# Ten hc tiles for the selective scan of images 1 to 3 where there were six, four of them in a second pool opened behind the last scan inputs

## The chip, the cores and the metric

The kernel runs on one core of one Trainium2 chip. The metric is the device time of one execution in microseconds. A core has five engines with their own queues, each of which runs its instructions in the order in which they were written into it: TensorE (PE; its weight loads are listed as PEld), VectorE (DVE), ScalarE (ACT), GpSimd (POOL) and SyncE (SP), which here only starts transfers. SBUF is the working memory, PSUM the memory that matmuls write to.

## What is computed

Four images of 64 x 64 tokens with 128 channels pass through four layers. Layer 0 is a selective scan block: layer norm, an input projection, a 3 x 3 depthwise convolution, then in each of four directions a recurrence over 4096 tokens for 256 channels x 16 states, and after it a norm, a gate, an output projection and an MLP. Layer 1 is attention of every token to every token, layer 2 a block of convolutions, layer 3 attention over a 7 x 7 neighbourhood and an MLP. The part of layer 0 that matters here:

```python
def step(h, t):
    x_t, d_t, B_t, C_t = t
    h = jnp.exp(d_t[..., None] * A) * h + (d_t * x_t)[..., None] * B_t[:, :, None, :]
    return (h, jnp.einsum('bkdn,bkn->bkd', h, C_t))
_, ys_l = jax.lax.scan(step, h0, scan_in)
```

## The kernel before

The program is written as plain loops, and a scheduler puts the instructions of each engine in order before the kernel runs. It does so with a planned time of its own and with priorities: the scan's instructions are traced under `priority(tc, K, SCAN_FIRST)` with a very large number, so that they come after whatever else is ready, and fill what the other layers leave free. The order is fixed in the program; on the chip each engine follows it and waits where an operand or a buffer is not ready.

`network` (L1624) first makes the scan's pools (`make_scan`, L410), then `scan_inputs` of image 0 (L277). Then come, for images 0 to 3, the scan of the image (`selective_scan`, L438) and beside it other work: beside the scan of image 0 the scan inputs of images 1 to 3, and beside the scan of image i (1 to 3) `rest` (L1594) of image i - 1, which is scan output (L565), layer 1 (L715), layer 2 (L911) and layer 3's attention (L1222). Layer 3's MLP of an image is run within the scan output of the next. `rest` of image 3 has no scan beside it and stands at the end; its scan output (`scan_over`) takes the space of the scan's pools.

The scan of one image runs over four directions (`ORDER`), eight chunks of 512 tokens, two halves of the channels, four groups of states (`j`) and two parts (`pp`). Each turn of the innermost loop is called a unit here: 512 units for an image, 2048 in all. For one unit:

- GpSimd makes `dB` (128 x 2 x 512) from `du` and a row of B (L485), into one of four tiles.
- ScalarE makes `dA = exp(dt * A)` twice (L491), into one of three PSUM banks.
- VectorE runs the recurrence twice (L493). Where the unit's number is in `ON_POOL`, it writes into the unit's `hc` tile, and GpSimd multiplies the tile by a row of C two units later (L506). Otherwise it writes over `dA`, and VectorE makes the product into `hc` (L498). For images 1 to 3, 7 of 16 units are GpSimd's.
- ScalarE keeps the last column as the state of the next chunk (L500, L502).
- PE sums the states: for each `j`, eight (as the trace counts them) passes `py <- hc, pick` for two units (L539), which read the two `hc` tiles and set them free. At the first `j` a matmul with `y_before` opens the sum (L524, L527, L534), at the last the sum is copied out of PSUM (L549, L556) before `py`, a single bank, can be opened again.

`hc` is a tile of 4 KB per partition; there are six. A seventh unit's recurrence or product must wait for a py matmul. The matmuls of the other layers stand between py matmuls on PE: in layer 1 the score and value matmuls (L781, L829), in layer 2 two blocks of five 3 x 3 convolutions (L247, called from layer 2), in layer 3 the scores (L1287, L1291) and the values and sums (L1307), in 64 groups an image, each opened by two L1287 instructions. In scan output they are L602 to L640.

Of the kernel before, what the change touches and what calls it, by code (L numbers as in the profile page):

```python
# [28 lines left out]
F32 = mybir.dt.float32  # L29
# [13 lines left out]
LC = 512  # L43
# [24 lines left out]
def mid(ap, n):  # L68

    return bc(ap.unsqueeze(1), [ap.shape[0], n, ap.shape[1]])  # L70
# [29 lines left out]
class Together:  # L100
# [3 lines left out]
    def __init__(self, tc, K):  # L104
        self.tc, self.K, self.done = tc, K, None
# [57 lines left out]
def loader(tc, pool, A, layer):  # L163
    def load(name, shape, src=None):
        t = pool.tile(shape, F32, name=f"w{layer}_{name}")
        tc.nc.sync.dma_start(t, A[f"L{layer}_conv_{name}"] if src is None else src)
        return t

    return load
# [95 lines left out]
def make_conv_diagonals(tc, K, A, out):  # L265
    nc = tc.nc
    with tc.tile_pool(name="mk_conv", bufs=1) as pool:
        convw = pool.tile([128, ND, 9], F32, name="convw")
        nc.sync.dma_start(convw, A["L0_conv_conv_w"])
        diag = pool.tile([128, ND, 9, 128], F32, name="conv_diag")  # L270
        for d in range(ND):
            for t in range(9):
                nc.scalar.activation(diag[:, d, t, :], K.ident, AF.Copy, scale=convw[:, d, t : t + 1])
        nc.sync.dma_start(out, diag)
# [135 lines left out]
def make_scan(ctx, tc, K, A):  # L410

    nc = tc.nc
    S = SimpleNamespace()
    big = ctx.enter_context(tc.tile_pool(name="ss_big", bufs=1))
    S.pool = ctx.enter_context(tc.tile_pool(name="ss", bufs=2))
    S.psum = ctx.enter_context(tc.tile_pool(name="ss_ps", bufs=1, space=PSUM))
    load = loader(tc, big, A, 0)
    S.A = load("A_log", [128, KD, NJS, NPR, 2])
    nc.scalar.activation(S.A, S.A, AF.Exp)
    nc.vector.tensor_scalar_mul(S.A, S.A, -1.0)  # L420
    ds4 = load("Ds", [128, ND, KD])
    total = big.tile([128, ND], F32, name="Dsum")
    nc.vector.tensor_reduce(total, ds4, AX.X, ALU.add)
    S.skip = big.tile([128, ND, 128], F32, name="skip_diag")
    for d in range(ND):
        nc.scalar.activation(S.skip[:, d, :], K.ident, AF.Copy, scale=total[:, d : d + 1])

    S.pick = big.tile([128, 32], F32, name="pick")
    nc.gpsimd.memset(S.pick, 1.0)
    for base, sign in ((0, 1), (3, -1)):  # L430
        nc.gpsimd.affine_select(
            S.pick, S.pick, [[-4 * sign, 32]], ALU.is_ge, 0.0, base=base, channel_multiplier=sign
        )
    S.unit = 0
    return S


def selective_scan(tc, K, S, D, img):  # L438
# [6 lines left out]


    nc = tc.nc
    pool, psum = S.pool, S.psum
    waiting = []

    def settle(unit):
        while waiting and waiting[0][0] <= unit:
            waiting.pop(0)[1]()

    for k in ORDER:
# [4 lines left out]
        for i in range(NCH):  # L460
            c = NCH - 1 - i if back else i
            for hf in range(2):
# [11 lines left out]
                for j in range(NJS):  # L474
# [7 lines left out]
                    for pp in range(2):  # L482
                        pr = 2 * hf + pp
                        dB = pool.tile([128, 2, LC], F32, name="dB", bufs=4)
                        nc.gpsimd.tensor_mul(dB, dus[pp], mid(bt, 2))  # L485
                        on_pool = S.unit % 16 in ON_POOL[img > 0]
                        S.unit += 1
                        hc = pool.tile([128, 2, LC], F32, name="hc", bufs=6)
                        for g in range(2):
                            dA = psum.tile([128, LC], F32, name="dA", bufs=3)  # L490
                            nc.scalar.activation(dA, dts[pp][:, g, :], AF.Exp, scale=S.A[:, k, j, pr, g : g + 1])  # L491
                            hg = hc[:, g, :] if on_pool else dA
                            nc.vector.tensor_tensor_scan(  # L493
                                hg[:, order], dA[:, order], dB[:, g, order],
                                0.0 if i == 0 else state[:, j, pr, g : g + 1], ALU.mult, ALU.add,
                            )
                            if not on_pool:
                                mm = nc.vector.tensor_mul(hc[:, g, :], dA, ct)  # L498
                                if i < NCH - 1:
                                    nc.scalar.copy(state[:, j, pr, g : g + 1], dA[:, last : last + 1])  # L500
                        if on_pool and i < NCH - 1:
                            nc.scalar.copy(state[:, j, pr, :], hc[:, :, last])  # L502
                        if on_pool:

                            def product(hc=hc, ct=ct, made=made):
                                made.append(nc.gpsimd.tensor_mul(hc, hc, mid(ct, 2)))  # L506

                            waiting.append((S.unit + BEHIND, product))
                        else:
                            made.append(mm)  # L510
                        hcs.append(hc)
                        settle(S.unit)
# [1111 lines left out]
def network(tc, A, out):  # L1624
    nc = tc.nc
    with ExitStack() as ctx:
        nc.scalar.preload_act_table_set("natural_log_exp_and_others")
        K = make_consts(ctx, tc)
        dram = ctx.enter_context(tc.tile_pool(name="scratch", bufs=1, space=DRAM))

        def scratch(name, shape):
            return dram.tile(shape, F32, name=f"{name}_dram")

        D = SimpleNamespace()
        D.bias = scratch("bias", [len(BIAS_KINDS), 128, HEADS * 512])
        D.biasT = [[scratch(f"biasT{k}_{i}", [128, HEADS, LC]) for i in range(4)] for k in range(3)]
        D.conv_diag = scratch("conv_diag", [128, ND, 9, 128])
        D.w2_diag, D.w2_norms = scratch("w2_diag", [128, 20, 128]), scratch("w2_norms", [128, len(NORMS2), 4])
        D.w2_cv4, D.w2_bias = scratch("w2_cv4", [128, 128]), scratch("w2_bias", [1, 128])
        for name, shape in (("sz", [128, ND, LC]), ("xc", [128, ND, LC]), ("y", [128, ND, LC])):  # L1640
            setattr(D, name, [[scratch(f"{name}{b}_{c}", shape) for c in range(NCH)] for b in range(B)])
        for name, shape in (("delta", [128, ND, LC]), ("du", [128, ND, LC]), ("bc", [NS, 2, LC])):
            made = [
                [[scratch(f"{name}{b}_{k}_{c}", shape) for c in range(NCH)] for k in range(KD)] for b in range(B)
            ]
            setattr(D, name, made)
        D.y_first = [[[scratch(f"y_first{b}_{k}_{c}", [128, ND, LC]) for c in range(NCH)] for k in range(2)] for b in range(B)]
        D.y_cols = [scratch(f"y_cols{b}", [NCH, 128, NCH, ND, RC * RC]) for b in range(B)]
        for name in ("x4", "x5"):
            setattr(D, name, [scratch(f"{name}_{b}", [NT, C]) for b in range(B)])  # L1650
        D.shift = [scratch(f"shift{b}", [NJ, 128]) for b in range(B)]

        with ExitStack() as scan_ctx:
            S = make_scan(scan_ctx, tc, K, A)
            make_conv_diagonals(tc, K, A, D.conv_diag)
            with priority(tc, K, SCAN_FIRST // 2):
                with tc.tile_pool(name="mk_w2", bufs=1, side="right") as pool:
                    make_layer2(tc, K, A, D, pool)
            scan_inputs(tc, K, A, D, 0)
            before = None  # L1660
            for img in range(B):
                with priority(tc, K, SCAN_FIRST):
                    selective_scan(tc, K, S, D, img)
                if img == 0:
                    make_bias(tc, K, A, D.biasT)
                    for later in range(1, B):
                        scan_inputs(tc, K, A, D, later)
                else:
                    rest(tc, K, A, D, img - 1, before)
                    before = img - 1, out[img - 1]  # L1670
            rest(tc, K, A, D, B - 1, before, scan_ctx.close)
            layer3_mlp_alone(tc, K, A, D, B - 1, out[B - 1], 8)
        needed = ctx.enter_context(tc.tile_pool(name="needed", bufs=1)).tile([1, 1], mybir.dt.int32, name="needed")
        bound_exceeded(tc, K, needed)
        with tc.If(nc.values_load(needed) > 0):
            everything_again(tc, K, A, D, out)
# [80 lines left out]
```

## Time and profile before

| | us |
|---|---|
| median of 3 runs | 8911.95 |
| lowest and highest run | 8906.75, 8919.55 |
| profiled execution, span | 8926.7 |
| PE busy in it | 7138.8 (80%) |
| VectorE busy | 7119.8 (80%) |
| GpSimd busy | 7048.6 (79%) |
| ScalarE busy | 5642.5 (63%) |

The span runs from the first to the last instruction of one execution that was taken with the profiler on; it is 15 us over the median of the runs. For the time of the profiled execution only this span is known. The scan of image 0 takes about the first 2200 us, that of each further image some 1850 us, the last py matmul is at 7804 us, and the rest of image 3 follows without GpSimd. GpSimd's share of 79% is therefore near 90% over the time in which it has work. In a row of a group the two numbers after the bar are the busy time in all (us) and the mean of one (ns), and what follows the second bar is how long the engine stood idle before them and what ended most of that. In a row of stretches the columns are the stretch, its length, the busy time and the count of instructions of PE, PEld, DVE, ACT and POOL, the mean granted clock of TensorE as a share of its full speed, the busy share of the DMA engines and GB/s.

### The profile page before, as it was taken

How to read it: one execution, taken by the hardware profiler on the slowest of the kernel's cores; microseconds unless marked ns; L12 is line 12 of the kernel's file. 1: busy time of each engine (PE TensorE's matmuls, PEld its weight loads, DVE VectorE, ACT ScalarE, POOL GpSimd, SP SyncE). 2: the span in 40 equal slices, each digit the busy share in tenths (PEclk: the TensorE clock that was granted, in tenths of full speed). 3: DMA queues.
4: the chain of work that ended last, by engine and by line, in shares of the span. 5: the costliest groups of instructions: out<-in, count | busy, mean ns of one | idle time of the engine just before them, and what ended most of it. 6: DMA issues, size and time to landing. Idle time of an engine off the chain costs nothing. (4 is left out here: it accounts for less than half of the span.)

```text
span 8926.7 us, 101201 instructions
## 1 busy us (share of the span) xinstructions
PE 7138.8 (80%) x30116; PEld 2711.7 (30%) x30116; DVE 7119.8 (80%) x8483; ACT 5642.5 (63%) x11581; POOL 7048.6 (79%) x3064
## 2 busy tenths in 40 slices
PE   6835868687788997887788988777888888888987
PEld 2211213132332232333322232333322333343333
DVE  3888878888899989998899989988999889813433
ACT  5646767676576666667766666657766666654355
POOL 5988898989899989998899979987899889900000
PEclk8756868697799998888899998888899988999989
DMA  5777676777554546566444555565544555520020
GB/s 174 249 236 239 227 252 239 266 240 266 188 168 165 170 150 222 188 205 201 164 165 164 179 180 195 191 208 171 166 167 169 169 198 194 173 69 4 7 79 29
DMA packets 864124, 1581.89 MB, mean 177 GB/s; under 512 B 219702, under 2 KB 344781, under 8 KB 859214
## 3 DMA queue, kind: packets, MB, share of 16 engines
q1 hardware_dynamic: 733261, 1399.17, 47.0%
q10 hardware_dynamic: 130304, 176.19, 5.5%
q8 instruction: 240, 3.93, 0.2%
q14 instruction: 319, 2.61, 0.1%
HBM read 1280.47 MB, written 283.59 MB: 175 GB/s over the span
## 5 line engine op out<-in xcount | busy, mean ns | idle before, releaser
L485 POOL TENSOR_TENSOR dB<-du,b_rows 128x1024 f32<-128x1024 f32 x2048 | 4801.3, 2368 | 622.9 <-DVE hc L493 184.8
L491 ACT ACTIVATE dA<-dt,w_A_log 128x512 f32<-128x512 f32 x4096 | 2784.7, 690 | 636.5 <-DVE hc L493 353.1
L493 DVE TENSOR_TENSOR_SCAN dA<-dA,state,dB 128x512 f32<-128x512 f32 x2128 | 2634.8, 1272 | 231.0 <-ACT dA L491 136.3
L493 DVE TENSOR_TENSOR_SCAN hc<-dA,state,dB 128x512 f32<-128x512 f32 x1456 | 1802.5, 1268 | 263.6 <-PE py L539 117.2
L506 POOL TENSOR_TENSOR hc<-hc,c_rows 128x1024 f32<-128x1024 f32 x832 | 1969.3, 2367 | 52.7 <-issue 23.9
L498 DVE TENSOR_TENSOR hc<-dA,c_rows 128x512 f32<-128x512 f32 x2432 | 1567.9, 676 | 115.0 <-PE py L539 97.5
L539 PE MATMUL py<-hc,pick 128*32 128x512 f32 x8192 | 1244.7, 686 | 367.3 <-POOL hc L506 270.7
L500 ACT COPY state<-dA 128x1 f32<-128x1 f32 x2128 | 327.5, 158 | 1220.4 <-DVE hc L498 1211.8
L829 PE MATMUL pa<-e,l_v 128*128 128x512 f32 x2048 | 1062.0, 650 | 16.8 <-ACT e L785 16.2
L781 PE MATMUL pair<-l_g,l_f 32*128 32x512 f32 x2048 | 530.5, 667 | 198.3 <-ACT e L785 146.9
L785 ACT ACTIVATE e<-pair 128x1024 f32<-128x1024 f32 (+1 forms) x448 | 508.4, 1135 | 225.7 <-PE pair L781 220.3
L829 PEld LDWEIGHTS pa<-e,l_v 128*128 128x128 f32 x2048 | 374.2, 199 | 668.5 <-issue 621.1
L539 PEld LDWEIGHTS py<-hc,pick 128*32 128x32 f32 x8192 | 209.5, 116 | 1114.7 <-issue 476.7
L247 PE MATMUL ps<-band,w_conv_diag 128*128 128x504 f32 (+3 forms) x1152 | 503.5, 596 | 6.7 <-ACT delta L397 6.5
L1287 PE MATMUL pair<-table,ident 128*128 128x512 f32 x768 | 414.3, 665 | 111.4 <-ACT e L1297 79.1
L493 DVE TENSOR_TENSOR_SCAN dA<-dA,dB 128x512 f32<-128x512 f32 x304 | 356.2, 1213 | 76.2 <-POOL dB L485 57.4
L328 POOL TENSOR_TENSOR du<-delta,xc 128x1024 f32<-128x1024 f32 x128 | 335.4, 2630 | 52.0 <-ACT delta L397 45.3
L1297 ACT ACTIVATE e<-pair 128x1024 f32<-128x1024 f32 (+1 forms) x224 | 254.3, 1135 | 155.6 <-PE pair L1291 155.6
L201 PE MATMUL ps<-ident,ln_xn 128*128 128x128 f32 x512 | 134.2, 360 | 263.9 <-ACT ln_xn L198 214.3
L219 PE MATMUL ps<-xnT,w_fc_w 128*128 128x512 f32 x512 | 266.6, 656 | 62.9 <-ACT xnT L202 22.7
L233 PE MATMUL ps<-mlp_h,w_fc_w 128*128 128x512 f32 x512 | 275.8, 683 | 42.6 <-ACT mlp_h L226 42.6
L247 PEld LDWEIGHTS ps<-band,w_conv_diag 128*128 128x128 f32 x1152 | 221.6, 194 | 288.7 <-issue 260.4
(274 smaller groups left out, 8400.0 us busy)
## 6 DMA issues: line engine op xcount, KB each, us to landing
b_rows<-bc_dram SPq DMA_DIRECT2D x1024, 256.0 KB
c_rows<-bc_dram SPq DMA_DIRECT2D x1024, 256.0 KB
dt<-delta_dram SPq DMA_DIRECT2D x512, 512.0 KB
du<-du_dram SPq DMA_DIRECT2D x512, 512.0 KB
delta_dram<-delta ACTq DMA_DIRECT2D x128, 512.0 KB
du_dram<-du SPq DMA_DIRECT2D x128, 512.0 KB
table<-biasT_dram SPq DMA_DIRECT2D x72, 512.0 KB
y_first_dram<-y_sum ACTq DMA_DIRECT2D x128, 256.0 KB
```

The lines of the kernel that those rows point to most:

```text
L247: mm = nc.tensor.matmul(out[:, r0 - row0 : r1 - row0, c0:c1], lhsT((dy + 1) * 3 + dx + 1), src[:, r0 + dy : r1 + dy, c0 + dx : c1 + dx], s ...
L328: nc.gpsimd.tensor_mul(du.rearrange("p d (a b) -> p d a b", b=H), deltas[b].rearrange("p d (a b) -> p d a b", b=H), tk,)
L485: nc.gpsimd.tensor_mul(dB, dus[pp], mid(bt, 2))
L491: nc.scalar.activation(dA, dts[pp][:, g, :], AF.Exp, scale=S.A[:, k, j, pr, g : g + 1])
L493: nc.vector.tensor_tensor_scan(hg[:, order], dA[:, order], dB[:, g, order], 0.0 if i == 0 else state[:, j, pr, g : g + 1], ALU.mult, ALU.add,)
L498: mm = nc.vector.tensor_mul(hc[:, g, :], dA, ct)
L506: made.append(nc.gpsimd.tensor_mul(hc, hc, mid(ct, 2)))
L539: mm = nc.tensor.matmul(py[0][32 * q : 32 * q + 32, :], S.pick, hcs[q // 2][:, q % 2, :], start=(k == 1 and j == 0), stop=(j == NJS - 1),)
L781: nc.tensor.matmul(ps[:, u, :], f[quad, t // 4, span(t % 4, 128)], g[quad, c, :], start=True, stop=True)
L785: made = nc.scalar.activation(e, ps, AF.Exp)
L829: nc.tensor.matmul(pa, v[:, 8 * q + t, :], es[q], start=(t == 0 and q == 0), stop=(t == 7 and q == 3),)
L1287: nc.tensor.matmul(ps[:, u, :], K.ident, t[:, u, :], start=True, stop=False)
```

## The change

The scan asks an object for its `hc` tiles. For the scan of image 0 and for the first 40 tiles of image 1, it takes them from the old ring of six. After that it takes four of every ten from a pool `ss_more`, opened after the scan inputs of image 3 have been traced and so at the address where their pools began, and six of every ten from the old ring; each tile is then used again ten units later. The pool stays open until the scan's other pools close, so that the pools of `rest` for images 0 to 2 start 16 KB per partition higher. The branch of the program that runs everything again in a general form does not use the second pool.

```diff
@@ make_scan
     S.unit = 0
+    S.products = Products(S.pool)
     return S
+class Products:
+
+    def __init__(self, pool):
+        self.pool, self.more, self.turn = pool, None, 0
+
+    def widen(self, pool, bufs):
+        self.more, self.bufs, self.turn = pool, bufs, -40
+
+    def tile(self):
+        self.turn += 1
+        if self.more is not None and self.turn > 0 and self.turn % (6 + self.bufs) < self.bufs:
+            return self.more.tile([128, 2, LC], F32, name="hc", bufs=self.bufs)
+        return self.pool.tile([128, 2, LC], F32, name="hc", bufs=6)
@@ selective_scan
-    pool, psum = S.pool, S.psum
+    pool, psum, products = S.pool, S.psum, S.products
...
-                        hc = pool.tile([128, 2, LC], F32, name="hc", bufs=6)
+                        hc = products.tile()
@@ network
                     for later in range(1, B):
                         scan_inputs(tc, K, A, D, later)
+                    more = scan_ctx.enter_context(tc.tile_pool(name="ss_more", bufs=1))
+                    S.products.widen(more, 4)
```

## The prediction

> **What bounds the kernel now.** I read the busy shares first, then the groups, then what VectorE waits for, then busy times cut at the stages of the layers that run beside the scan, and last the timeline of one such stage and of the scan's end. The page's span and its costliest groups of the scan:
>
> ```profile
> span 8926.7 us, 101201 instructions
> ...
> L485 POOL TENSOR_TENSOR dB<-du,b_rows 128x1024 f32<-128x1024 f32 x2048 | 4801.3, 2368 | 622.9 <-DVE hc L493 184.8
> ...
> L506 POOL TENSOR_TENSOR hc<-hc,c_rows 128x1024 f32<-128x1024 f32 x832 | 1969.3, 2367 | 52.7 <-issue 23.9
> ```
>
> A scan unit (one dB, one hc tile) costs GpSimd one L485 and, in 7 of 16 units for images 1 to 3, one L506: 2.368 + 7/16 x 2.367 = 3.40 us. The waits that the change aims at, over the whole run (microseconds, times, longest):
>
> ```profile
> DVE hc L493 <- PE py L539: 118.8, 67, 6.3
> ...
> DVE hc L498 <- PE py L539: 97.5, 48, 8.1
> ```
>
> Asked stage by stage, images 1 to 3 hold 134 us of these 216, and 124 of the 134 lie beside layer 1 (60) and layer 3 (64). What GpSimd does there is the next view: busy time of PE, PEld, DVE, ACT and POOL in stretches cut at the stages (layer 1, layer 2, layer 3 of image 0; scan output of image 1; layer 3 of image 2 up to the last py matmul).
>
> ```profile
> 2540.00:3245.00 705.00, 628.65 (x2642) 194.61 (x2640) 663.33 (x704) 474.58 (x897) 699.18 (x302) 0.96 0.51 172
> 3245.00:3385.00 140.00, 131.53 (x444) 56.64 (x444) 109.05 (x136) 85.91 (x171) 89.97 (x40) 0.95 0.39 124
> 3385.00:4000.00 615.00, 500.08 (x2712) 183.46 (x2712) 562.33 (x640) 391.08 (x834) 596.87 (x258) 0.86 0.63 207
> 4000.00:4445.00 445.00, 340.94 (x1336) 162.10 (x1336) 379.67 (x535) 318.98 (x710) 359.62 (x156) 0.83 0.55 180
> ...
> 7225.00:7804.00 579.00, 468.72 (x2536) 177.24 (x2536) 534.27 (x613) 365.35 (x768) 557.99 (x241) 0.86 0.60 200
> ```
>
> GpSimd is 99% busy beside layer 1 and 97% beside layer 3: there a VectorE wait for an hc tile costs nothing, since the next dB is not there anyway. It idles beside layer 2 (50 of 140 us) and scan output (85 of 445). Layer 2's gaps, GpSimd and then PE in order of time (start, length, idle before in brackets):
>
> ```profile
> 3305.03 4.72 POOL L485 TENSOR_TENSOR dB<-du,b_rows 128x1024 f32<-128x1024 f32 x2 [20.34 <-DVE hc L493]
> ...
> 3343.45 2.36 POOL L485 TENSOR_TENSOR dB<-du,b_rows 128x1024 f32<-128x1024 f32 x1 [21.00 <-PE ps L979]
> ```
>
> ```profile
> 3264.62 32.16 PE L247 MATMUL ps<-l_h,w_diag 128*128 128x448 f32 x90
> ```
>
> Twice a stage (the second time from 3304.72) PE runs 32 us of convolution with no py matmul, so no hc tile comes free, the scan stops, and GpSimd stands for 20 us. This happens six times. The run's end, PE:
>
> ```profile
> 7823.58 1.98 PE L1287 MATMUL pair<-table,ident 128*128 128x512 f32 x4 [1.12 <-ACT e L1297]
> ...
> 7828.41 1.98 PE L1287 MATMUL pair<-table,ident 128*128 128x512 f32 x4
> ...
> 7836.66 1.16 PE L1324 MATMUL pj<-w_proj_w,oT 128*128 128x128 f32 x8 [0.26 <-DVE oT L1320]
> 7851.09 6.50 PE L602 MATMUL ps<-y,center 128*128 128x512 f32 x8 [13.27 <-DMA y<-y_dram]
> ```
>
> Layer 3 of image 2 ends at 7838, 34 us after the last py matmul, and only then does the tail begin (its weights and y are loaded into space that this layer 3 held): 8927 - 7838 = 1089 us that the change does not touch. So the end is the end of layer 3 of image 2, plus a constant.
>
> **The Trainium skill.** "Perfetto Trace Analysis", section Optimization Strategy, says that a gap repeating on the engine that should be saturated can mean that there isn't enough SBUF or PSUM for the next tile. The trace agrees in layer 2 (six gaps of about 20 us), and shows in the other stages that a wait for a tile on another engine than the bound is no such gap. The same page, Sequencer Loop, has each instruction wait in its engine's queue; the trace agrees: py matmuls stand behind 90 convolution passes. "GPSIMD Engine Reference", section 3.1, gives 4497 ns for a GpSimd and 2293 ns for a VectorE product of 2048 f32; here 2367 ns for 1024 against 2 x 676 for VectorE's L498, so GpSimd is indeed the dear side of the unit.
>
> **The change part by part.** It adds and removes no arithmetic. The first 40 hc tiles of image 1 are as before. The new pool lies where the scan inputs' pools lay, but their last matmul stands ahead of unit 512 on PE, and its first tile comes at unit 553: no wait; taken as 0. The pools of the later layers move up by 16 KB per partition; layer 3's last e tile then shares space with xT, whose last read (layer 2) comes before: 0.
>
> What does change is the planned order. I counted, in both built programs, how many scan units stand before each stage's first instruction on ScalarE (before / after): layer 1 of image 0 starts 597/596.5; layer 2 805/808.5, ends 829/838; scan output of image 1 1014.5/1024.5, ends 1115/1124.5; layer 2 1327.5/1339 to 1351/1367.5; scan output of image 2 1540/1557 to 1638/1659; layer 2 1855.5/1876.5 to 1879/1903.5; scan ends at 2048 in both. So the scan is planned ahead of the layers by 24.5 units at the end. And after the last py matmul PE has 6 groups of layer 3's 64 (two L1287 instructions each) before, 16 after.
>
> Price by stage:
>
> - Layer 1 and layer 3, GpSimd-bound, 3.43 us per unit (3.40 / 0.99): layer 1 +4, +2, 0 units; layer 3 +1, +0.5, -24.5: -17 units, -58 us. Counted on PE it is +6, +2, +4, +2, 0, -24: -10 units, -34 us. ScalarE's count sets when an exponential may run, PE's when a py matmul may; I take the middle, -46.
> - Layer 2: +5.5, +5, +3.5 units at no GpSimd time, hidden by the 20 us gaps. But PE is 94% busy there. Its extra py matmuls are 5 units x 0.53 us (1.06 us for the 8 passes of two units), and in four of the six convolutions a y_before matmul now stands behind the first 9 or more of 45 instructions, 1.1 us and an unknown wait for the last y_sum copy: from 0 to 8 us. I take 4 us a stage, +12; ends 0 and +36.
> - Scan output: -0.5, -0.5, +4 units. GpSimd is 81% busy here; what orders the stage is ScalarE and VectorE between layers' steps (VectorE's hc waits are only 7 us in the three). Free at best, 3 x 3.40 = 10 at worst; I take +5.
> - Layer 3's hc waits, 64 us: nearly all covered by GpSimd. Its idle time there is some 20 us a stage; I take -5; ends -12 and 0.
> - Left of layer 3 after the scan: 10 groups more. Two starts of one above are 4.83 us apart, the pair before 4.16: 4.5 us, so 45; with one chunk's q, k, v and two ends of chunks, on paths now uncovered, about 9 more: +54; ends +45 and +65. Beside the scan the same group took 615 / 64 = 9.6 us, but cost nothing, as GpSimd set the pace.
>
> Sum: -46 + 12 + 5 - 5 + 54 = +20 us. Against the profiled span, 8926.7 + 20 = 8947; the runs' median, 8912, is 15 us (0.16%) under that span, so 8932. All ends together: -58 + 0 + 0 - 12 + 45 = -25 and -34 + 36 + 10 + 0 + 65 = +77.
>
> **Rivals.** (1) Gaps filled for nothing, ends faster. The place is layer 2: 14 units run inside its six convolutions, the stage stays at 140 us, the scan is done 58 + 12 us early, and the 16 left groups cost only their 45: -25, 8887. For it: GpSimd's and VectorE's 31 and 50 us of idle time in that stage. Against: PE is full there, and the scan's lead must be paid in layer 3 left over. It decides if the last py matmul comes more than 54 us earlier. (2) A draw: the 124 us of waits under a full GpSimd were never paid, and lead and leftover cancel within 18 us: 8912. For it: my two counts differ by 24 us, as much as the result. (3) Broken convolutions: the y_before matmuls inside wait for ScalarE's copy and stall PE in a stage that it bounds, +36 in place of +12, and the shorter lead counted on PE holds: +56, 8968. For it: L527 already waits 36 us for y_sum copies. Against: copies are planned before. (4) The change does nothing since the new tiles come late: excluded from unit 553 on by the count above.
>
> **How the numbers follow.** Forecast, slower by 10 to 40 us: 0.36. Rival 3 and beyond: 0.12. Draw: 0.29. Rival 1: 0.21. Rival 4: 0.02. About 0.2%, 18 us, is what a measurement can tell. Slower by more than that: most of the forecast's case and all of rival 3, 0.45; faster, 0.22 (rival 1 and a little beyond); within, the draw, rival 4 and the forecast's low edge, 0.33. The likeliest case gives 8932; the range takes in rival 1's 8887 and rival 3's 8968: 8885 to 8972. The likeliest case's own range is 8922 to 8952.
>
> **What would show it.** In the profile after: the 20 us gaps of GpSimd in layer 2 shorter than 12 us; layer 1 and layer 3 still with GpSimd above 96%; the waits for py on VectorE mostly gone with no gain from it; the last py matmul 20 to 45 us earlier; and layer 3 of image 2 running 80 to 100 us past it instead of 34, with 1089 us behind. I am wrong if layer 3's leftover is short, if GpSimd's idle time in scan output falls, or if layer 2 grows by over 10 us.

## The result and the profile after

The change makes the kernel faster by a fifth of a per cent: 8898.9 us median of 20 runs (8888.4 to 8915.7), against 8916.9 us for the kernel before beside it (20 runs, 8906.8 to 8946.4). The ratio is 0.9977, 95% interval 0.9970 to 0.9984. The forecast was 8932 us. The profiled execution is the slowest of the 20, 16.8 us over their median; its span is 12.7 us under that of before.

Lines of the kernel after are 16 higher from L485 on (dB L501, recurrence L509, VectorE's product L514, GpSimd's product L522, py L555, layer 3's scores L1303). The page after, span and the scan's two groups of GpSimd:

```profile
span 8914.0 us, 101143 instructions
...
L501 POOL TENSOR_TENSOR dB<-du,b_rows 128x1024 f32<-128x1024 f32 x2048 | 4817.8, 2389 | 553.6 <-DVE hc L509 137.0
...
L522 POOL TENSOR_TENSOR hc<-hc,c_rows 128x1024 f32<-128x1024 f32 x832 | 1988.6, 2390 | 34.7 <-issue 16.1
```

What VectorE waits for, after (us, times, longest):

```profile
DVE hc L514 <- PE py L555: 61.1, 19, 8.2
...
DVE hc L509 <- PE py L555: 26.4, 9, 6.3
```

The waits for tiles fell from 216 to 88 us. To see which of that counted, I cut both traces at the first TensorE instruction of each stage (L602, L749, L950, L1249 of the kernel before) and read the busy times between the cuts. GpSimd idles for a row's length less the fifth busy time. First the kernel before: layer 3 of image 0, layer 3 of image 2 up to the last py matmul, and the rest up to the start of image 3's scan output.

```profile
3383.60:4018.30 634.70, 509.69 (x2750) 186.59 (x2750) 581.99 (x662) 399.64 (x848) 613.95 (x266) 0.86 0.63 206
...
7228.40:7804.40 576.00, 469.12 (x2537) 177.35 (x2538) 530.87 (x610) 363.20 (x763) 554.75 (x240) 0.87 0.60 200
7804.40:7851.10 46.70, 29.02 (x165) 10.79 (x165) 2.42 (x6) 7.96 (x9) 0.00 (x0) 0.88 0.21 58
```

And after: layers 1, 2 and 3 of image 0, the scan output of image 1, and the last two as above.

```profile
2570.10:3271.20 701.10, 628.91 (x2616) 192.07 (x2617) 664.45 (x708) 468.12 (x893) 698.21 (x303) 0.94 0.53 172
3271.20:3415.50 144.30, 133.91 (x469) 58.14 (x470) 125.15 (x150) 93.47 (x189) 110.71 (x48) 0.97 0.48 154
3415.50:4040.30 624.80, 494.87 (x2744) 185.29 (x2745) 582.22 (x664) 396.63 (x834) 615.21 (x267) 0.87 0.65 210
4040.30:4461.30 421.00, 326.21 (x1310) 159.61 (x1311) 360.26 (x516) 315.10 (x716) 344.22 (x149) 0.84 0.55 181
7223.20:7709.30 486.10, 394.95 (x2112) 145.56 (x2112) 454.01 (x521) 309.64 (x646) 473.63 (x205) 0.85 0.60 198
7709.30:7829.70 120.40, 86.61 (x486) 36.82 (x487) 6.32 (x18) 26.41 (x39) 0.00 (x0) 0.85 0.22 65
```

Three things are to be seen. Layer 3 of image 0 holds as much GpSimd work as before (614 and 615 us), and takes 10 us less: its idle time went from 21 to 10 us. In layer 3 of image 2 the scan ends 95 us earlier (7804 to 7709). And of these 95 us, 74 are given back at once: the rest of layer 3, with nothing of GpSimd beside it, grows from 47 to 120 us.

As GpSimd's work in all is constant (7049 and 7044 us up to there), the start of image 3's scan output is that work plus GpSimd's idle time. All stages of the three images together, idle us of GpSimd:

| | before | after |
|---|---|---|
| up to the first scan output | 289.6 | 297.0 |
| scan output | 223.6 | 218.4 |
| layer 1 | 21.6 | 12.7 |
| layer 2 | 150.9 | 109.1 |
| layer 3 beside the scan | 70.0 | 28.6 |
| layer 3 left over after the scan | 46.7 | 120.4 |
| sum | 802.4 | 786.2 |
| scan output of image 3 starts | 7851.1 | 7829.7 |

So the change takes 97 us of idle time away in four kinds of stage, and adds 74 at the end and 7 before the first scan output. The short stalls that went in layer 3 can be seen in what GpSimd waits for there; image 1, before and then after:

```profile
POOL dB L485 <- DVE hc L493: 10.9, 3, 8.1
POOL dB L485 <- issue: 4.4, 1, 4.4
POOL hc L506 <- issue: 3.8, 1, 3.8
POOL hc L506 <- ACT state L502: 2.6, 1, 2.6
```

```profile
POOL dB L501 <- DMA sz<-sz_dram: 2.7, 1, 2.7
POOL dB L501 <- DVE hc L509: 2.1, 2, 1.2
POOL dB L501 <- DMA b_rows<-bc_dram: 1.5, 1, 1.5
```

Two of these stalls, 4.4 and 3.8 us, come right after waits of VectorE for py (4.7 and 3.7 us): with six tiles a late py matmul holds VectorE's recurrence up, and GpSimd stands until that is done. The longest, 8.1 us, is of another kind: VectorE stood before a MEMSET of the next scan output (L584). VectorE and GpSimd in order of time:

```profile
5817.85 2.46 DVE L493 TENSOR_TENSOR_SCAN hc<-dA,state,dB 128x512 f32<-128x512 f32 x2 [4.68 <-PE py L539]
...
5820.44 2.36 POOL L485 TENSOR_TENSOR dB<-du,b_rows 128x1024 f32<-128x1024 f32 x1 [4.42 <-issue]
...
5929.29 0.27 DVE L584 MEMSET center<- 128x256 f32 x1 [8.92 <-issue]
...
5933.91 2.35 POOL L485 TENSOR_TENSOR dB<-du,b_rows 128x1024 f32<-128x1024 f32 x1 [8.13 <-DVE hc L493]
```

The idle times named "issue" have no releaser in the profile. Over the three layers 3, the idle time of GpSimd that lies under a wait of VectorE for py, or begins within 3 us of its end, is 22 of the 70 us before and none of the 29 after; in the layers 1 it is 6 of 22 and none of 13. So some 28 of the 50 us that went stood beside the waits that the change aims at. The other 22 went elsewhere in these stages, in part at their ends; these traces don't show by what.

What is paid at the end, TensorE after the last py matmul of the kernel after:

```profile
7710.84 0.51 PE L1323 MATMUL den<-e,ones 128*32 128x192 f32 x8
7712.06 1.12 PE L1338 MATMUL pj<-bias_row,ones 1*128 1x512 f32 x2 [0.71 <-ACT rec L1333]
...
7723.72 1.63 PE L201 MATMUL ps<-ident,ln_xn 128*128 128x128 f32 x4 [5.50 <-ACT ln_xn L198]
...
7734.10 3.78 PE L1303 MATMUL pair<-table,ident 128*128 128x512 f32 x4 [0.67 <-ACT v L1297]
...
7814.46 1.16 PE L1340 MATMUL pj<-w_proj_w,oT 128*128 128x128 f32 x8 [0.26 <-DVE oT L1336]
7829.71 2.90 PE L618 MATMUL ps<-y,center 128*128 128x512 f32 x3 [14.10 <-DMA y<-y_dram]
```

Sixteen groups of layer 3 are left (64 passes of L1303, four a group, fall after the last py matmul; 24, so six groups, before). Between 7711 and 7734 stands one chunk's layer norm and its q, k and v, which the scan covered before.

### The profile page after: what moved, and what is told of

It reads as the page before. It is cut to its first block, busy times and chain, and to the rows that moved or that the text cites. A ratio compares the mean times of both kernels' runs of the same rounds, so it can differ in the third digit from the quotient of the medians.

```text
span 8914.0 us, 101143 instructions
## 1 busy us (share of the span) xinstructions
PE 7120.9 (80%) x30116; PEld 2708.4 (30%) x30116; DVE 7132.4 (80%) x8483; ACT 5640.4 (63%) x11581; POOL 7043.5 (79%) x3064
## 5 line engine op out<-in xcount | busy, mean ns | idle before, releaser
L501 POOL TENSOR_TENSOR dB<-du,b_rows 128x1024 f32<-128x1024 f32 x2048 | 4817.8, 2389 | 553.6 <-DVE hc L509 137.0
L509 DVE TENSOR_TENSOR_SCAN dA<-dA,state,dB 128x512 f32<-128x512 f32 x2128 | 2634.8, 1275 | 242.6 <-POOL dB L501 129.4
L522 POOL TENSOR_TENSOR hc<-hc,c_rows 128x1024 f32<-128x1024 f32 x832 | 1988.6, 2390 | 34.7 <-issue 16.1
L509 DVE TENSOR_TENSOR_SCAN hc<-dA,state,dB 128x512 f32<-128x512 f32 x1456 | 1805.4, 1270 | 218.8 <-ACT dA L507 134.6
L514 DVE TENSOR_TENSOR hc<-dA,c_rows 128x512 f32<-128x512 f32 x2432 | 1568.2, 679 | 76.1 <-PE py L555 61.1
L555 PE MATMUL py<-hc,pick 128*32 128x512 f32 x8192 | 1244.2, 685 | 380.2 <-POOL hc L522 307.3
L555 PEld LDWEIGHTS py<-hc,pick 128*32 128x32 f32 x8192 | 211.5, 116 | 1147.5 <-issue 466.4
L1303 PE MATMUL pair<-table,ident 128*128 128x512 f32 x768 | 398.9, 644 | 97.2 <-ACT e L1313 76.5
L509 DVE TENSOR_TENSOR_SCAN dA<-dA,dB 128x512 f32<-128x512 f32 x304 | 356.8, 1215 | 75.6 <-POOL dB L501 62.3
L797 PEld LDWEIGHTS pair<-l_g,l_f 32*128 32x128 f32 x2048 | 139.0, 188 | 537.6 <-ACT e L801 275.0
```

What stands on the lines that cost most here:

```text
L509: nc.vector.tensor_tensor_scan(hg[:, order], dA[:, order], dB[:, g, order], 0.0 if i == 0 else state[:, j, pr, g : g + 1], ALU.mult, ALU.add,)
L555: mm = nc.tensor.matmul(py[0][32 * q : 32 * q + 32, :], S.pick, hcs[q // 2][:, q % 2, :], start=(k == 1 and j == 0), stop=(j == NJS - 1),)
L797: nc.tensor.matmul(ps[:, u, :], f[quad, t // 4, span(t % 4, 128)], g[quad, c, :], start=True, stop=True)
L1303: nc.tensor.matmul(ps[:, u, :], K.ident, t[:, u, :], start=True, stop=False)
```

## Theories

Layer 2's filled gaps and layer 3's lost stalls come together in the change. Theory A: the gain is the stalls of layers 1 and 3 (50 us), while units moved into layer 2 come back as layer 3 left over. Theory B: the gain is layer 2's idle time, filled with more units. A third, L, was formed after the first four runs. In all kernels below the whole computation is done; only the tiles of the `hc` rings, the share of GpSimd or a priority differ.

## Ten tiles in some stages only

The ring of ten is used only while the number of the unit lies in a list; elsewhere the old six serve.

```diff
+L2_UNITS = (range(795, 850), range(1318, 1372), range(1846, 1908))
...
-        if self.more is not None and self.turn > 0 and self.turn % (6 + self.bufs) < self.bufs:
+        near = any(512 + 40 + self.turn in r for r in L2_UNITS)
+        if self.more is not None and near and self.turn % (6 + self.bufs) < self.bufs:
```

> Ten tiles only for the units around layer 2 of images 0, 1 and 2, six everywhere else: by the kernel's order layer 2 holds 30, 30 and 31 units where 24, 23.5 and 23.5 were, as in the change. Theory A (the gain is the short GpSimd stalls of layers 1 and 3 that deeper buffers take away, 9 and 41 us by the traces, while units moved into layer 2 come back as layer 3 left over after the scan): nothing, 8905 to 8925 us, ratio 0.999 to 1.001, with GpSimd's idle time in the layers 3 at 60 to 70 us as before, against 29 with the change. Theory B (the gain is the idle time of layer 2, filled with 19 more units): the whole gain of the change or more, some -20 us, ratio 0.9975 to 0.998.

The complement has `self.turn > 0 and not near` in the last line:

> The complement: ten tiles in images 1 to 3 except for the units around layer 2, where six stay. By the kernel's order the layers hold the units that they held before, and some 7 groups of layer 3 are left after the scan, where 8 were before and 18 with the change. Theory A: all of the slack and nothing given back, -30 to -50 us, ratio 0.9945 to 0.9966, with 25 to 35 us of GpSimd idle time in the layers 3 (70 before). Theory B: nothing, ratio 0.999 to 1.001, since layer 2 keeps its gaps of 150 us.

Layer 2 alone: 8873.1 us, ratio 0.9944 (0.9931 to 0.9958). All but layer 2: 8883.2 us, ratio 0.9951 (0.9937 to 0.9965). Each half is better than the whole change. The first in stretches, layer 2 of image 0, scan output of image 1, and the left over part:

```profile
3233.80:3374.60 140.80, 132.38 (x469) 57.28 (x470) 126.06 (x151) 94.25 (x190) 113.20 (x49) 0.98 0.48 156
4014.60:4428.70 414.10, 315.70 (x1276) 158.70 (x1277) 345.98 (x501) 304.61 (x688) 329.31 (x142) 0.85 0.53 175
...
7729.40:7794.30 64.90, 47.03 (x290) 19.29 (x289) 3.79 (x8) 13.27 (x15) 0.00 (x0) 0.92 0.20 59
```

Layer 2 holds 100 units in the three images, 20 more than before (dB products started between the cuts), and is 8.9 us longer: 0.4 us a unit. The scan outputs hold 12 fewer and are 38 us shorter, 3.2 us a unit. So B is right in kind, and A falls as the only cause; B's size was too small, since it was taken from the change, which has 14 units more in layer 2 and none fewer in scan output.

The second in the layer 3 of image 0 and in the part left over:

```profile
3417.30:4036.80 619.50, 506.37 (x2743) 186.63 (x2743) 582.72 (x656) 392.86 (x838) 611.94 (x265) 0.86 0.64 212
...
7766.70:7813.50 46.80, 28.98 (x166) 10.97 (x165) 2.42 (x6) 7.95 (x9) 0.00 (x0) 0.85 0.20 54
```

The work is that of before (612 and 614 us), the stage is 15 us shorter, and the part left over is unchanged. Over the three images layer 3's idle time falls from 70 to 33.5 us with no unit moved into layer 2, as A expected. This one number refutes the 5 us (12 at most) that the prediction expected layer 3 to give. It is not all waits for hc tiles: the part that stands beside VectorE's waits for py, counted as above, falls from 22 to 13 us. How much of the fall is the ring itself and how much the order that the scheduler writes for a deeper ring stays open; ten tiles in the order of before were not tried on the chip.

## A ring of eight, and less work for GpSimd

```diff
-                    S.products.widen(more, 4)
+                    S.products.widen(more, 2)
```

> Eight tiles where the change has ten (two of them in the second pool). By the kernel's order as many units lie in layer 2 (28.5, 28 and 27.5) and 20 groups of layer 3 are left over. Theory A: the slack that two more tiles give is between that of six and of ten, the leftover that of the change: -5 to -15 us, ratio 0.9983 to 0.9995, GpSimd idle in the layers 3 between 30 and 65 us. Theory B: the same as the change, ratio 0.9975 to 0.998, since the units in layer 2 are nearly the same.

8913.8 us, ratio 0.9988 (0.9982 to 0.9995): A's range. But its idle sum is that of the change (787 us) and its scan output of image 3 starts within 2 us of it; the part left over is 127 us. That the medians lie 15 us apart is no contradiction: the traces are single executions, that of the change 16.8 us over its median, that of eight 6.0 us over its own, so that one trace of each doesn't settle a difference of this size.

```diff
-ON_POOL = ((1, 4, 7, 10, 13), (0, 2, 4, 6, 9, 11, 13))
+ON_POOL = ((1, 4, 7, 10, 13, 17, 20, 23, 26, 29), (0, 2, 4, 6, 9, 11, 13, 16, 19, 21, 24, 26, 29))
...
-                        on_pool = S.unit % 16 in ON_POOL[img > 0]
+                        on_pool = S.unit % 32 in ON_POOL[img > 0]
```

> The change with 13 of 32 of the scan's units for images 1 to 3 on GpSimd, where 14 of 32 are (one unit in 32 goes over to VectorE, the work as a whole is the same). In layers 1 and 3 GpSimd is over 96% busy with the change and VectorE some 93 to 95%. Theory A: GpSimd's work per unit sets the pace there, 3.43 us per unit; one unit in 32 less of its work (2.39 us a product) is 0.075 us per unit off, over some 1200 units in those layers -60 to -90 us on the end of the scan, of which more leftover of layer 3 gives back half to two thirds: 8860 to 8890 us, ratio 0.9935 to 0.9965. Theory C (VectorE is as near its own bound, and takes the place at once): 0 to -10 us against the change, ratio 0.9965 to 0.9985.

8904.5 us, ratio 0.9982 (0.9974 to 0.9990): no gain over the change, and outside A's range. The number lies in C's range, but C's reason, that VectorE holds the scan at its old pace, is not what the trace shows, for the scan does end earlier, by 72 us (layer 3 of image 2 up to the last py matmul, and the rest):

```profile
7231.60:7637.20 405.60, 327.84 (x1754) 121.07 (x1754) 386.27 (x448) 261.47 (x564) 388.76 (x168) 0.84 0.59 202
7637.20:7814.40 177.20, 126.91 (x744) 54.81 (x740) 8.85 (x28) 41.63 (x64) 0.00 (x0) 0.88 0.15 46
```

The part left over takes 57 of the 72 us. That gave theory L: what the scan is ahead by when layer 2 of image 2 ends is paid as layer 3 left over, near 2.9 us a unit. A unit taken out of a layer 3 saves about 3.4 us (before, image 0: 634.7 us for 184 units); out of the last one it therefore saves almost nothing. A unit put into layer 2 must be taken from a scan output before, where it is worth 3.2 us.

## The lead and where it is handed back

Three kernels differ from that with ten tiles around layer 2 only in the list of units. The lists of the one whose lead is released, of the one with six tiles in scan output, and of the one with six at the end:

```diff
+TEN = (range(795, 1016), range(1318, 1540), range(1846, 1940),)
...
+TEN = (range(600, 1000), range(1121, 1530), range(1646, 2100),)
...
+TEN = (range(553, 1908),)
```

> Ten tiles around layer 2 and in layer 3 of images 0 and 1 until shortly before their end, and around layer 2 and the start of layer 3 of image 2; six in the scan-output stages, in layer 1 and at the end. Theory L (the lead that the scan holds at the end of layer 2 of image 2 is paid as layer 3 left over, some 2.9 us per unit by the runs so far, so that units put into layer 2 gain only where the scan output takes up the lead before): the order has 1887.5 units done there, as the run with ten tiles around layer 2 alone, so layer 3 left over is 65 to 75 us; layer 2 keeps 85 to 95 us of GpSimd idle time, layer 3 falls to 35 to 45 us: 8840 to 8862 us, ratio 0.991 to 0.9935, the best so far. Theory S (the gains of layer 2 and of layer 3 are the same gain, and do not add): 8870 to 8890 us as the two runs that had one of them.

8873.6 us, ratio 0.9949 (0.9935 to 0.9963): the part left over is 66.1 us as L said, layer 3's idle time 26.6 us, under what it said; but layer 1's rose to 38 us and layer 2 kept 102. The time is in the range of S, so the stalls seem to have moved here; only the lower end of the interval, 0.9935, touches L's range.

> The change with six tiles in the scan-output stages (and some 15 units before each), ten in layers 1, 2 and 3. Theory L: the lead is taken up there, the scan output of images 0, 1 and 2 is 8 to 14 us shorter each than before, 1894 units are done at the end of layer 2 of image 2 by the order (1903.5 with the change, 1879 before), layer 3 left over is 80 to 95 us instead of 120, and the time 8860 to 8880 us, ratio 0.993 to 0.9955. Rival R (layer 3 left over comes of ten tiles in the last layer 3, whatever lead the scan brings): left over 115 to 130 us and 8895 to 8905 us as the change.

8876.9 us, ratio 0.9950 (0.9938 to 0.9963), left over 84.1 us: L, and not R. The scan outputs are 20 us shorter in sum, not 8 to 14 each (the third is not shorter at all).

> The change with ten tiles until the end of layer 2 of image 2 and six after it, so that the last layer 3 runs with six. Theory L: the lead is there already (1903.5 units done at the end of that layer 2 by the order, as with the change), layer 3 left over stays at 105 to 120 us and the time within 10 us of the change: 8893 to 8910 us, ratio 0.9972 to 0.999. Rival R: with six tiles in the last layer 3 the left over part falls to 50 to 70 us and the time to 8845 to 8870 us.

8900.1 us, ratio 0.9975 (0.9965 to 0.9986), left over 111.6 us: L, and R is out. The last layer 3 with six tiles ends as the one with ten; the bill was there before it began. From the last py matmul to the scan output of image 3, first the trace with six tiles in scan output, then that with six at the end:

```profile
7711.40:7795.50 84.10, 63.12 (x401) 26.58 (x401) 3.79 (x8) 17.36 (x19) 0.00 (x0) 0.93 0.24 71
```

```profile
7711.20:7822.80 111.60, 79.83 (x442) 33.77 (x443) 4.94 (x16) 25.16 (x36) 0.00 (x0) 0.86 0.21 66
```

In both the scan ends at the same 7711 us, and yet one is 27 us ahead of the other. The end of the scan is not the measure.

## A much larger lead

With six tiles, as before, the sums are given the scan's priority:

```diff
-                            mm = nc.tensor.matmul(
-                                py[0][32 * q : 32 * q + 32, :], S.pick, hcs[q // 2][:, q % 2, :],
-                                start=(k == 1 and j == 0), stop=(j == NJS - 1),
-                            )
+                            with priority(tc, K, -SCAN_FIRST):
+                                mm = nc.tensor.matmul(
+                                    py[0][32 * q : 32 * q + 32, :], S.pick, hcs[q // 2][:, q % 2, :],
+                                    start=(k == 1 and j == 0), stop=(j == NJS - 1),
+                                )
```

> The kernel before, six tiles, with the sums over the states (the matmuls of py) put at the scan's own high priority, so that hc tiles come free early and by the order the scan runs 40 to 74 units ahead of where it was, with 34 groups of layer 3 left after it. Theory L: the last py ends 150 to 210 us earlier than before (7804 us), layer 3 left over is 230 to 290 us (some 2.9 us for each of 74 units on top of 47), and the time is 8890 to 8940 us, ratio 0.996 to 1.002: no gain for a scan that ends a whole 150 us or more earlier. Rival (an earlier end of the scan is an earlier end, as the prediction's first rival had it): 8780 to 8850 us.

9071.8 us, ratio 1.0167 (1.0154 to 1.0180): outside both. The stretch up to the first scan output, layer 3 of image 2, and the part left over:

```profile
0.00:2382.90 2382.90, 1582.77 (x4951) 528.61 (x4951) 1894.52 (x2211) 1495.40 (x3392) 2100.30 (x932) 0.75 0.69 236
7422.20:7747.30 325.10, 255.88 (x1367) 96.27 (x1367) 299.10 (x346) 205.33 (x435) 309.32 (x134) 0.86 0.58 197
7747.30:7992.00 244.70, 179.49 (x1004) 77.86 (x1004) 11.37 (x38) 57.70 (x89) 0.00 (x0) 0.86 0.12 36
```

The left over part, 244.7 us, is in the range that L gave. What L's sum had as free was the lead itself: the first 38 units were done before the first scan output, which now starts 120 us later (2383 instead of 2263), 3.2 us each, at unchanged idle time (283 and 290 us). The last py matmul thus came 57 us earlier and not 150 to 210. So a lead can be paid twice, in full when it is won and by 2.7 us a unit at the end: the scan output of image 3 starts 141 us later than before (7992 against 7851). The layers 3 beside the scan are 263 us shorter, but 120 us are added before the first scan output, 86 in the scan outputs and layers 1 and 2, and 198 at the end.

## A version better than both

If L holds, ten tiles should serve wherever the lead is handed back before the last layer 3, and six around layer 2 of image 2. Two lists, no lead a and no lead b:

```diff
+TEN = (range(600, 960), range(1121, 1490), range(1646, 1846), range(1908, 2100),)
...
+TEN = (range(700, 960), range(1221, 1490), range(1746, 1846), range(1908, 2100),)
```

> Ten tiles in layers 1 and 3 and in layer 2 of images 0 and 1, six in the scan-output stages, for some 55 units before each of them, and around layer 2 of image 2. By the order the scan has 1879 units done at the end of layer 2 of image 2, exactly where it was before, and 8 groups of layer 3 are left over as before. Theory L: nothing is paid at the end (left over 43 to 55 us), GpSimd idles 115 to 130 us in layer 2 (151 before), 25 to 40 us in layer 3 (70), 15 to 40 us in layer 1 (22): 8850 to 8870 us, ratio 0.992 to 0.9945, the best of all by 5 to 15 us. Theory S (stalls taken from one stage turn up in another, as in the run that widened layer 3 and saw layer 1 stall more): 8872 to 8885 us, as the others.

> As the run beside it, with the six-tile stretches reaching 100 units into each layer 1, so that by the order layer 2 of images 0 and 1 holds 30 and 30.5 units (27 and 29.5 beside it) and that of image 2 holds 21 (23.5); 1882 units are done at its end and 7 groups are left over. Theory L: within 8 us of the run beside it, 8848 to 8872 us, layer 1 with some 10 us more idle time and layer 2 with 5 to 10 us less. Theory S: 8872 to 8885 us.

8850.3 us, ratio 0.9921 (0.9907 to 0.9934), and 8851.4 us, ratio 0.9924 (0.9910 to 0.9937): the first at the lower edge of L's range, the second within it, both outside S. The first in layer 2 and layer 3 of image 0, scan output of image 1, and at the end:

```profile
3242.40:3385.90 143.50, 131.90 (x452) 56.77 (x452) 119.34 (x145) 91.63 (x184) 105.00 (x46) 0.97 0.43 140
3385.90:4018.30 632.40, 515.33 (x2767) 188.37 (x2767) 588.22 (x670) 400.50 (x851) 619.93 (x268) 0.85 0.63 211
4018.30:4432.80 414.50, 315.06 (x1280) 158.32 (x1282) 346.56 (x501) 305.55 (x689) 329.99 (x142) 0.85 0.53 175
...
7738.30:7778.70 40.40, 22.96 (x119) 8.26 (x118) 2.42 (x6) 6.93 (x8) 0.00 (x0) 0.85 0.22 63
```

Layer 2 takes 10 units more than before, the scan outputs 13 fewer, layer 3 four more, and 40 us are left over. The first run's finer figures were missed on both sides: layer 3's idle time is 43.7 us (25 to 40 expected), layer 1's 13.6 (15 to 40), the part left over 40.4 (43 to 55). The second run's finer expectation, less idle time in layer 2 than in the first, failed (114.3 against 114.7 us).

All kernels side by side; the kernel before, run beside each group of them, had medians of 8916.9 to 8923.4 us, so that the ratios above are the comparison. "Units in layer 2" counts the dB products that start there, "done" those that have ended when layer 2 of image 2 ends; idle times are GpSimd's, in us, over three images, and "all idle" takes in the stretch up to the first scan output. All columns but the median are of one profiled execution each, which ran from 15 us under to 17 us over the median.

| kernel | median us | units in layer 2 | idle layer 2 | idle layer 3 | done | left over | all idle |
|---|---|---|---|---|---|---|---|
| before | 8916.9 | 80 | 150.9 | 70.0 | 1882 | 46.7 | 802 |
| the change | 8898.9 | 94 | 109.1 | 28.6 | 1906 | 120.4 | 786 |
| layer 2 only | 8873.1 | 100 | 84.4 | 60.0 | 1889 | 64.9 | 749 |
| all but layer 2 | 8883.2 | 80 | 153.1 | 33.5 | 1878 | 46.8 | 768 |
| eight | 8913.8 | 94 | 118.4 | 34.7 | 1910 | 127.0 | 787 |
| thirteen of 32 | 8904.5 | 95 | 121.7 | 39.3 | 1929 | 177.2 | 875 |
| released | 8873.6 | 94 | 101.8 | 26.6 | 1890 | 66.1 | 754 |
| six in scan output | 8876.9 | 96 | 104.4 | 21.3 | 1897 | 84.1 | 752 |
| six at end | 8900.1 | 94 | 104.6 | 38.3 | 1906 | 111.6 | 778 |
| sums first | 9071.8 | 106 | 82.6 | 69.6 | 1956 | 244.8 | 944 |
| no lead a | 8850.3 | 90 | 114.7 | 43.7 | 1882 | 40.4 | 735 |
| no lead b | 8851.4 | 91 | 114.3 | 37.9 | 1886 | 37.5 | 720 |

The left over part follows the units done: from 1882 to 1956 it grows by 198 us, 2.7 a unit, and the others lie within 20 us of that line. (Thirteen of 32 has 48 products of L522 fewer, 114 us at 2.38 us each, and by the trace 104 us less busy time of GpSimd than the change, so that its idle sum doesn't compare with the others.)

## Why the prediction was wrong

It summed to +20 us at the end of layer 3 of image 2; the traces show -21.4 us at the start of the scan output that follows. Its terms against the stretches:

| step of the prediction | taken | shown |
|---|---|---|
| the stages' start | 0 | +4.6 |
| units in and out of layers 1 and 3 | -46 | -66 |
| layer 2 | +12 | +12.8 |
| scan output | +5 | +4.0 |
| layer 3's hc waits (shown: idle time of layers 1 and 3) | -5 | -50 |
| left of layer 3 after the scan | +54 | +73.7 |
| sum | +20 | -21 |

- "Layer 3's hc waits, 64 us: nearly all covered by GpSimd" is the step that failed. GpSimd was called full at 97%, but 3% of 1860 us in three layers 3 is 56 us by the rounded share and 70 us by the rows, over three times the whole forecast of +20. Of them 41 us went, and 9 of layer 1's 22. The run with ten tiles everywhere but at layer 2 showed 36.5 of the 41 alone. Covered was right for most of the 124 us of waits: some 28 us of GpSimd's idle time stood beside them and went. The other 22 us that went were idle time of these stages that the prediction left standing. The end of -12 was no bound: the prediction itself named 20 us a stage, 60 in all.
- "I take the middle, -46": the ScalarE count (-17 units) was nearer than the PE count (-10). Between the cuts, layer 1 holds 7 units more and layer 3 22 fewer, -15; GpSimd's busy time there changes by +15.5 and -81.7 us, in sum more than either count gave.
- Layer 2 was right in its units, 14 moved in as counted. That +12.8 us agree with the +12 is luck in part: the three stages grew by 6.4, 10.2 and -3.8 us where 4 each were taken. (Scan output likewise: +4.0 is the sum of 11.3, -7.2 and -0.1.) The gaps went from 20 to 11 and 15 us in image 0, so "shorter than 12" held for one of two. The convolutions are cut in two by a y_before matmul (L543), and no long stall stands between the parts:

```profile
3288.26 9.68 PE L247 MATMUL ps<-l_h,w_diag 128*128 128x448 f32 x18 [1.54 <-DVE l_h L957]
3297.78 1.02 PE L543 MATMUL py<-y_before,ident 128*128 128x512 f32 x2
3298.64 25.68 PE L247 MATMUL ps<-l_h,w_diag 128*128 128x448 f32 x72
...
3332.74 6.54 PE L247 MATMUL ps<-l_h,w_diag 128*128 128x448 f32 x18
3339.11 1.02 PE L543 MATMUL py<-y_before,ident 128*128 128x512 f32 x2
3339.97 25.68 PE L247 MATMUL ps<-l_h,w_diag 128*128 128x448 f32 x72
```

  This excludes rival 3, whose +36 needed them. (L527's waits for copies of y_sum, which it named as 36 us, are 36 behind L556 and another 31 behind L549.)
- The left over part was mis-sized: the ten groups more, as counted, took 48 us (7734.1 to 7782.0) where 45 were taken; but the end of one chunk and the norm, q, k and v of the next took 25 us from the last py matmul to 7734.1, not "about 9". The six groups that follow take 48 us, 47 before.
- Rival 1 (8887) named the right side and its own test, a last py matmul more than 54 us earlier (it is 95), but not the cause: layer 2 did not stay at 140 us, the left over part did not cost only 45, and the difference came from layer 3's idle time. (Its idle times for layer 2 are the wrong way round: by the row shown they are 50 us for GpSimd and 31 for VectorE.) Rival 2's reason, waits never paid, is refuted for some 28 of the 124 us; its other half, lead and left over part cancelling within 18 us, held, with -66 against +74.
- Of the signs by which it would be seen to be wrong, two appeared: scan output's idle time fell, by 5 us, and layer 2 grew by over 10 us. Both terms had been taken right in their sums; they were not where it failed.
- "1089 us that the change does not touch" holds only roughly: from the start of image 3's scan output on, the trace after takes 1084.3 us and that before 1075.6, so that the span fell by 12.7 us and not by 21.4. Over the twelve traces this part takes 1070 to 1087 us; TensorE's mean granted clock in it is 0.92 in the two longest, with eight tiles and with thirteen of 32, and 0.94 in no lead a with 1069.8 us. Whether the change has a part in it stays open.
- "Perfetto Trace Analysis", section Optimization Strategy, on a repeating gap on the engine that should be saturated, was read as applying only to layer 2's 20 us gaps. The page speaks of the same gap repeating; in layer 3 the stalls beside waits for a tile were scattered, up to 4.4 us long and 22 us in all, and they counted as well.

## What to carry to other kernels

An engine that is 97% busy over a long stage still has room: turn the share into microseconds before you call a wait covered, and compare it with the size of the effect that you forecast. Where a scan and a stream of other work share a core, the end is the bound engine's work plus its idle time in all stages, the part after its last instruction included; a lead pays only if it is taken up in a stage where a unit costs much, before the end. Deep buffers are worth having in the stages with gaps, and cost where they only let one stream run away from the other.

## Not expected of the hardware

GpSimd's products look slower in the trace after (2389 against 2368 ns), and are not: where one follows another at once, the median from start to start over the whole trace is 2.314 us before and 2.313 after. Where they follow each other closely in layer 2, the record of one is 2.64 us long, while the starts lie 2.31 us apart, so that the records overlap:

```profile
3270.23 2.64 POOL L501 TENSOR_TENSOR dB<-du,b_rows 128x1024 f32<-128x1024 f32 x1
3272.54 2.64 POOL L522 TENSOR_TENSOR hc<-hc,c_rows 128x1024 f32<-128x1024 f32 x1
3274.85 4.97 POOL L501 TENSOR_TENSOR dB<-du,b_rows 128x1024 f32<-128x1024 f32 x2
```

The Trainium skill's "Perfetto Trace Analysis", section GPSIMD Engine Instruction, calls such spans unreliable and has one time them by the spacing of their starts; the trace agrees, with 2.31 us here and also where the records are 2.36 us long. The prediction's 3.40 us a unit, made from recorded means, is 3.32 by the spacing (2.31 x 23/16); layer 1 of image 0 before, 206 units in 691.6 us, has 3.36.
